# Two diffusion blocks on one core: new due times for the instruction planner, and two unread products at TensorE's start

## The chip, the cores and the metric

The kernel runs on one core of a Trainium2 chip. The metric is the device time of one execution in microseconds. A core has five engines that run side by side, each with its own queue of instructions in a fixed order: TensorE (PE in the profile; PEld is its weight load), VectorE (DVE), ScalarE (ACT), GpSimd (POOL) and SyncE (SP), which here only issues transfers. They wait for one another through semaphores. TensorE writes its products into eight banks of PSUM, called W here; VectorE and ScalarE read them from there.

## The reference

For each of 16 images of 256 tokens with 256 channels, two transformer blocks are computed in float32, one after the other. Shortened:

```python
# block 1: three residual parts, each modulated by m = silu(cond) @ w_ada + b_ada
h = ln(x) * (1 + sc_msa) + sh_msa
x = x + g_msa * self_attention(h)        # windows of 128 tokens, shifted by 64, 16 heads of 16
h = ln(x) * (1 + sc_mca) + sh_mca
x = x + g_mca * topk_cross(h, ctx)       # softmax over the 16 largest of 256 scores
h = ln(x) * (1 + sc_mlp) + sh_mlp
x = x + g_mlp * (silu(a) * b @ w_m2 + b_m2)      # a, b = halves of h @ w_m1 + b_m1, 1024 each
# block 2: cross attention, both sides normalized and modulated by cond
q = (ada_ln(x, ctx_cond, Wss_q) @ Wq + bq); k, v = ada_ln(ctx, ctx_cond, Wss_kv) @ Wkv + bkv
out = x + softmax(q k^T / 4) v @ Wp + bp
```

The outputs are the 16 images of 256 x 256.

## The kernel before

All weights are loaded once and stay on chip. At the start the conditioning vectors are turned into scales, shifts and gate rows: `conditioned` loads `cond`, makes silu of it on ScalarE and VectorE, turns it with TensorE (line 704) and copies it into the tile `condT`; `ada_columns` multiplies pieces of `w_ada`, which are loaded into tiles named `rest`, with it (line 721) and adds the bias (lines 727 and 729, VectorE); `gate_rows` does the same for the gate rows (lines 742 and 762), which go to memory and come back per image (line 394). `biases` loads the bias vectors and turns them into columns (line 678, copied by VectorE at 679).

Then each image passes through five stages, named by tags: `self` (self attention), `prep` (keys, values and queries of the top-k attention), `topk`, `mlp`, and `last` (block 2). Work of neighbouring images is mixed: while VectorE looks for the 16 largest scores of one image, TensorE works on the feed-forward part of the image before and on the self attention of the image after.

The lines that the prediction speaks of: normalization by `normalized` (BN statistics at 442 and 444 on VectorE, three small operations and the scaling into `xn` on GpSimd at 449 to 454), turned to channel-major at 466 (TensorE) and modulated at 480 (ScalarE) into `xT`; products of `xT` with weights at 492 and 528; self attention scores at 798, their maxima at 605 (VectorE), sent by sixteen small transfers into the query tile at 622 (SyncE, from the transposed maxima `nmT`), scores again at 806, exponentials at 629 (ScalarE), products with the values at 598, division at 555 to 558, back to channel-major at 565, projection at 575 with weights that were multiplied with the gate row at 421 (GpSimd, `gw`). A round of the top-k attention (there are four per image) has scores at 845 into four banks; VectorE then takes, per bank, the eight largest (MAX8, 864), removes them (872), takes the next eight (884) and removes them (889); ScalarE makes exponentials (877), GpSimd multiplies (893) into `prT`, and TensorE turns this at 542 for the product with the values at 598. The feed-forward part is 906 to 933, block 2's scores are 950 and 962.

TensorE takes three kinds of work, with 128, 32 or 33 rows or columns at a time (the `mode` of an operation): 798, 806, 845, 950 and 962 are of the second kind, 598 of the third, the rest of the first.

The order of every engine's instructions is decided before the kernel is built. Each operation has a due time, from the table `DUE` by tag and by its number in the tag, to which the image's number is added. The class `Plan` sorts all operations by due time, hands out tiles and banks in that order, and emits them. The tags `topk`, `self`, `prep`, `last` and `mlp` have one table each for all middle images, so the order there repeats from image to image. The planner also follows a rough time of each engine; where it expects TensorE to wait for over a microsecond, it puts in fillers, which are products of the identity matrix with itself into a free bank that nobody reads:

```python
            if o.eng == "PE" and t - free["PE"] > IDLE and free["PE"]:
                ...
                n = int((t - max(free["PE"], ok[0][0]) - 0.15) / FILLER) if ok else 0
```

What stands ahead of the plan (the identity matrix, masks for even and odd heads made from it, and tiles set to fixed values) is put into the queues by the framework's own scheduler.

Of the kernel before, what the change touches and what calls it, by code (L numbers as in the profile page):

```python
# [12 lines left out]
ALU = mybir.AluOpType  # L13
# [3 lines left out]
P = 128  # L17
# [17 lines left out]
        -9079, -9474, -9247, -7795, -10959, -5686, -7231, -10933, -5595, -5764, -7671, -10944, -8055, -6777, -10987,  # L35
        -8081, -7859, -719, -437, -438, -481, -6999, -7280, -511, -720, -536, -6808, -436, -8602, -467, -7346, -144,
        -528, -1472, -8696, -179, -78, -9103, -26, -462, -493, -574, -8606, 35, 199, -2104, 292, -47, 992, 1098, 1338,
        -644, 26, -8994, -144, 52, 10, -8772, -241, -8701, 551, 74, 19, 1012, -516, -8708, 29, 1085, 1257, -514, -452,
        -6996, 1627, 1833, 1607, 911, 1468, 582, -843, -8601, 1445, 486,
    ),  # L40
    "self0": (
        -199, -1161, -7107, -1119, -1199, -1060, -1485, -9186, -125, -11006, -9245, -9080, -1563, -9248, -3868, -1470,
        -9200, -1606, -6831, -7277, -7299, -7349, -1217, -6958, -8697, -6883, -8698, -8665, -312, -310, -2158, -3486,
        -3338, -3035, -3750, -1684, -9048, -7290, -1182, -7290, -2158, -3339, -3752, -3826, -3561, -128, -8903, -9100,
        -1236, -8924, 9, -4022, -51,
    ),
    "prep0": (
        -524, -3251, -614, -3532, -3488, 354, -2949, 516, -8780, -39, -37, 80, 196, -3410, 569, -100, -3471,
    ),
    "topk0": (  # L50
        338, 282, 143, 7, -2799, -24, 100, -98, -2853, -35, 73, -8610, -2853, -8623, 112, -8616, -3052, -8436, -261,
        148, 579, -3006, -8621, -8749, 142, 439, -2809, 383, 324, 558, 726, -3356, -8631, -8719, 484, 172, -2951, 700,
        959, 1002, 919, 1061, 392, -8453, 550, -8714, -3364, 156, -461, 619, -3499, -8620, 551, 18, -2986, -61, 600,
        525, 700, 764, 725, 748, 690, -3352, 906, 842, 826, 553, 724, -72, 621, 835, 742, -3579, 803, 913, 816, 1073,
        821, 1081, 1074, 1309, 1219, 1329, 523, 620, 786, 1012, -3363, 1018, 801, 909, -3366, 958, 747, 1071, -3580,
        914, 791, 1170, -3634, 1022, 1024, 929, 1074, 820, 1013, 1016, 882, 1086, 819, 1181, 1178, 1255, 1240, 907,
        1133, 1169, 1256, 1239, 356, 1199, 1303, 1172, 1160, 1328, 1014, 1043, 1101, 1277, -3653, 1038, 1200, 1248,
        409, 1104, 1256, 1284, 352, 1060, 1143, 1107, 820, 1126, 1125, 1086, 972, 1307, 1262, 1260, 1197, 1206, 350,
        1052, 1246, 1188, 1311, 44, 1162, 1262, 1203, 1208, 1113, 1319, 1173, 1303, 1217, 1329, 677, 1356, 1398, 1437,
    ),  # L60
    "self1": (
        -4802, -987, -890, -482, -9103, -2047, -2146, -2225, -1549, -4844, -830, -1228, -5196, -3811, -1470, -4841,
        -4773, -861, -3828, -878, -800, -795, -794, -10252, -1021, -10208, -10029, -9854, -9854, -780, -807, -1214,
        -647, -4386, -4386, -4444, -3942, -602, -1053, -474, -328, -94, -659, -4237, -4066, -4401, -4387, -598, -1062,
        -270, -247, -15, 68, -4369, -213,
    ),
    "prep1": (
        -771, -5058, 71, -4579, -15, -331, -4364, 378, 34, 220, 223, 231, 182, -29, 145, 237, 302,
    ),
    "topk": (  # L70
        75, 3, 189, 110, 62, 3, -90, 2, 110, -39, 146, -53, -991, -146, 143, -62, -955, 353, 414, 558, 675, -104, 128,
        193, 253, 480, -914, 242, 339, 417, 490, -137, 393, 516, 407, 576, 134, 697, 349, 735, 402, 1049, 530, 279,
        443, -349, 556, 186, 562, 282, 1, 362, 587, 185, 11, 298, 611, 223, 479, 184, 179, 630, 712, -106, 253, 325,
        663, 746, 44, 673, 676, 706, 802, 580, 536, 739, 373, 857, 761, 882, 688, 894, 661, 942, 689, 837, 737, 833,
        885, 737, 799, 832, 902, 347, 344, 704, 30, 337, 331, 643, 725, 836, 941, 190, 1036, 1011, 826, 838, 232,
        1029, 960, 745, 776, 746, 903, 907, 736, 760, 415, 902, 909, 1090, 853, 1036, 1144, 1150, 894, 940, 677, 1028,
        721, 964, 206, 947, 922, 899, 675, 1026, 1075, 934, 678, 824, 918, 1039, 1051, 810, 1113, 1056, 691, 992, 779,
        1040, 959, 1033, 1027, 1116, 1109, 854, 1034, 1034, 999, 1107, 1008, 1160, 1027, 956, 1194, 1085, 501, 1236,
        1061, 1158,
    ),  # L80
    "self": (
        -1974, -677, -761, -758, -1718, -1767, -1387, -1242, -787, -1974, -758, -688, -1415, -1974, -694, -590, -601,
        -589, -1833, -538, -566, -1347, -1349, -1348, -345, -418, -466, -472, -473, -465, -226, -194, -253, -935,
        -969, -968, -425, -138, -335, -332, -197, -113, -150, -1139, -298, -295, -227, -133, -256, -227, -162, -70,
        -86, -126, -322,
    ),
    "prep": (
        -13, -197, -211, 5, 112, 57, 324, -19, -554, -568, -220, -220, -131, 617, 6, 17,
    ),
    "last": (  # L90
        1013, 1044, 1117, 1178, 1185, 1226, 6, 1311, 1060, 579, 1353, 1396, 2041, 1826, 1981, 1931, 2094, 1980, 2195,
        2146, 2088, 2131, 2195, 2090, 2231, 1173, 1171, 2258, 2182, 2188, 2187, 2280, 2286, 2324, 2285, 2351, 2342,
        2323, 2365, 2397, 2127, 2172, 2174, 2173, 2438, 2020, 2436, 1144, 1120, 1010, 1009, 2491, 2276, 2527, 2557,
        2522, 1882, 1284, 1283, 1388, 2589, 2220, 2310, 2627, 2557, 2593, 2591, 2133, 2518, 2425, 2647, 2528, 2649,
        2630, 2660, 2404, 2402, 2518, 2500, 2696, 2346, 2343, 2729, 2753, 2837, 2026, 2507, 2778,
    ),
    "mlp": (
        1668, 1326, 1271, 1268, 1484, 1490, 263, 1703, 1600, 1470, 1499, 1559, 1526, 1674, 1632, 1661, 1535, 959, 187,
        1556, 1289, 1565, 387, 1576, 1568, 1509, 398, 1568, 1257, 1602, 1505, 1616, 1614, 1238, 1421, 1717, 1041,
        1735, 1238, 1735, 1861, 1881, 1096, 1599, 1507, 1509, 1880, 1847, 1806, 859, 1648, 1897, 1712, 1861, 1529,  # L100
        1236, 1674, 882, 881, 1669, 1488, 1497, 847, 1474, 1745, 1088, 1027, 1748, 1027, 1396, 1020, 1336, 1944, 1978,
        1824, 2000, 1827,
    ),
    "self15": (
        -1762, -523, -14014, -616, -1736, -1651, -1652, -1042, -1147, -1738, -740, -1095, -1898, -709, -1266, -1267,
        -714, -1266, -347, -461, -328, -681, -998, -682, -328, -692, -173, -199, -712, -536, -370, -134, -249, -135,
        -196, -91, -162, -473, -302, -550, -648, -122, -354, -338, -167, -311, -83, -133, -766, -1659, -1733, -391,
        -316, -531, -392, -89, -90, -132, 9, -79, -1091, 38, -156, 56, 66, 20, 13, -2, -161, 241, -708, 238, -329,
        -330, -707, -708, 285, 291, 352, 224, 380, 268, -316, 172, -317, 101, 373, 359, 179, 337, 398, 481, 119, 495,
    ),  # L110
    "prep15": (
        -222, -967, 42, -45, -151, 164, 74, 16, -18, -558, -561, -12, -92, 162, 74, -25, 404, 542, 547, 120, 490, 572,
        643, 502,
    ),
    "topk15": (
        92, -80, 136, -123, 133, 163, 171, 196, 78, -109, 193, -109, -1023, 159, 130, 159, 158, 168, 185, 236, 271,
        94, 359, 360, 220, 427, -879, 398, 395, 509, 539, 549, 225, 229, 239, 315, 98, 643, 334, 674, 696, 1147, 445,
        592, 580, 515, 622, 396, 473, 393, 135, 439, 492, 151, -117, 197, 491, 200, -720, 603, 393, 670, 731, 644,
        587, 467, 498, 747, 808, 512, 590, 633, 676, 688, 392, 652, 737, 918, 876, 1071, 1261, 1573, -3159, 1602, 662,
        649, 517, 806, 441, 730, 751, 594, 825, 557, 651, 683, 892, 1122, 220, 963, 926, 822, 821, 246, 1476, 1180,  # L120
        657, 1112, 340, 1069, 1260, 833, 878, 299, 1088, 1346, 1180, 703, 174, 1401, 1346, 1595, 1790, 1787, -3140,
        1762, 890, 977, 706, 952, 896, 1190, 230, 1298, 1524, 1092, 707, 1667, 1501, 877, 345, 1190, 1191, 950, 1150,
        486, 1439, 1557, 1723, 1722, -2841, 1673, 2223, 1608, 1749, -2985, 1586, 2177, 693, 1028, 120, 1674, 1645,
        2210, 2346, 2345, -3151, 2194,
    ),
    "last15": (
# [39 lines left out]
LAG = {"PE": 0.22, "DVE": 0.14, "ACT": 0.18, "POOL": 0.1}  # L166

IDLE, FILLER = 1.0, 0.87
ISSUE, BEGIN, LAND, RATE, OPEN = 0.53, 0.9, 0.4, 320.0, 8


class Buf:
# [941 lines left out]
```

## Time and profile before

| | us |
|---|---|
| median of 3 runs | 1350.14 (1349.22 to 1350.87) |
| the profiled execution | 1350.46 |
| its span, first to last instruction | 1348.6 |
| TensorE busy | 1323.5 |
| VectorE busy | 1217.5 |
| GpSimd busy | 1020.9 |
| ScalarE busy | 1014.2 |
| fillers (line 353), 15 in the program, 30 records | 18.3 |

A group in the profile is read as line, engine, operation, output and inputs, sizes, and count. [...] Busy times of matmuls overlap at their ends; so the time from one group's start to the next group's start is the better measure of what a group costs. In brackets behind an instruction stands how long its engine had been idle before it, and what ended that. The fraction after the engines' busy times in a view of stretches is the granted clock of TensorE.

### The profile page before, as it was taken

The page shows a single profiled execution, that of the slowest core. Times are in us where ns is not written, and L with a number is a line of the kernel's source. Part 1 is how long each engine was busy: PE and PEld are TensorE (multiplying, and loading weights), DVE is VectorE, ACT ScalarE, POOL GpSimd, SP SyncE. Part 2 cuts the span into 40 slices and gives each one's busy share as a digit, 9 for nine tenths or more (in the row PEclk, how much of TensorE's full clock was granted, in tenths as well). Part 3 has the DMA queues.
Part 4 walks back from the last instruction along what each step waited for, and adds up shares of the span by engine and source line. Part 5 has one row for each costly group of instructions (what it writes and reads, how often), then busy time and mean ns, then how long its engine had stood idle before and what let it go on. Part 6 is the DMA issues. An engine that isn't in the chain of part 4 may idle for free.

```text
span 1348.6 us, 38673 instructions
## 1 busy us (share of the span) xinstructions
PE 1323.5 (98%) x13494; PEld 1033.3 (77%) x13494; DVE 1217.5 (90%) x4358; ACT 1014.2 (75%) x2359; POOL 1020.9 (76%) x1552
## 2 busy tenths in 40 slices
PE   8889999999999999999999999999999999999998
PEld 6557787878778787887878788787878778787785
DVE  4699999999999999999999999999999999998844
ACT  4356779787887978778787777878777787978774
POOL 1377887879688787968878796887869788877962
PEclk9889999999999999999999999999999999999999
DMA  5430010101001010100101010010101000000000
GB/s 157 139 109 10 26 41 11 41 17 33 18 18 41 11 40 18 34 17 19 41 11 38 20 34 18 18 41 11 38 20 34 18 27 17 18 18 2 17 2 18
DMA packets 64161, 42.45 MB, mean 31 GB/s; under 512 B 37763, under 2 KB 56751, under 8 KB 63711
## 3 DMA queue, kind: packets, MB, share of 16 engines
q1 hardware_dynamic: 63967, 39.99, 10.7%
q8 instruction: 107, 1.75, 0.6%
q14 instruction: 87, 0.71, 0.2%
HBM read 35.14 MB, written 4.29 MB: 29 GB/s over the span
## 4 chain that ended last, share of the span: by engine, by line
PE 92%; DVE 3%; SPq 1%; issue 1%; DMA 1%; ACT 1%; POOL 0%; POOLq 0%; DVEq 0%; ACTq 0%
PE W L906 17%; PE W L492 12%; PE W L598 11%; PE W L542 8%; PE W L933 8%; PE W L528 6%; PE W L575 6%; PE W L950 5%; PE W L845 5%; PE W L962 5%; PE W L466 3%; PE W L806 2%; PE W L798 2%; SPq L622 1%; DVE rest L872 1%
## 5 line engine op out<-in xcount | busy, mean ns | idle before, releaser
L893 POOL TENSOR_TENSOR prT<-rest,prT 128x512 f32<-128x512 f32 x256 | 325.0, 1273 | 75.0 <-DVE rest L889 73.5
L605 DVE TENSOR_REDUCE nm<-W 128x2 f32<-128x512 f32 (+1 forms) x384 | 239.9, 682 | 30.9 <-PE W L798 17.4
L877 ACT ACTIVATE prT<-W,ntop 128x256 f32<-128x256 f32 x512 | 214.2, 491 | 52.2 <-POOL ntop L866 38.8
L906 PE MATMUL W<-xT,w_L_xcond_w_m 128*128 128x256 f32 (+1 forms) x1088 | 249.1, 373 | 0.0
L629 ACT ACTIVATE pTO<-W 128x512 f32<-128x512 f32 (+1 forms) x392 | 198.8, 596 | 41.9 <-PE W L962 28.9
L906 PEld LDWEIGHTS W<-xT,w_L_xcond_w_m 128*128 128x128 f32 x1088 | 187.6, 190 | 52.3 <-ACT pTO L629 10.6
L872 DVE MATCH_REPLACE8 rest<-top,W 128x256 f32<-128x256 f32 x512 | 209.0, 419 | 0.0
L889 DVE MATCH_REPLACE8 rest<-top,rest 128x256 f32<-128x256 f32 x512 | 206.7, 416 | 0.0
L864 DVE MAX8 top<-W 128x8 f32<-128x256 f32 x512 | 190.1, 420 | 15.7 <-PE W L845 12.8
L884 DVE MAX8 top<-rest 128x8 f32<-128x256 f32 x512 | 190.7, 418 | 0.0
L545 ACT ACTIVATE pTT<-W 128x512 f32<-128x512 f32 x256 | 148.7, 622 | 17.2 <-PE W L542 15.2
L542 PE MATMUL W<-ident,prT 128*128 128x128 f32 x1024 | 145.2, 277 | 4.4 <-ACT k L514 1.7
L542 PEld LDWEIGHTS W<-ident,prT 128*128 128x128 f32 x1024 | 117.9, 142 | 27.9 <-issue 6.2
L923 POOL TENSOR_TENSOR mb<-ma,mb 128x256 f32<-128x256 f32 (+1 forms) x136 | 94.8, 697 | 40.1 <-ACT mb L921 24.4
L558 POOL TENSOR_TENSOR on<-tr,rec 128x128 f32<-128x128 f32 (+1 forms) x162 | 71.0, 443 | 67.8 <-DVE rec L557 67.5
L933 PE MATMUL W<-w_L_xcond_w_m,h 128*128 128x256 f32 x512 | 113.7, 379 | 0.0
L933 PEld LDWEIGHTS W<-w_L_xcond_w_m,h 128*128 128x128 f32 x512 | 97.0, 190 | 13.7 <-POOL x L416 0.3
L555 DVE STREAM_TRANSPOSE tr<-W 128x256 f32<-128x256 f32 (+1 forms) x162 | 78.4, 485 | 29.6 <-PE W L598 15.6
L598 PE MATMUL W<-pTO,v 128*17 128x128 f32 (+1 forms) x2112 | 102.2, 323 | 0.0
L926 POOL TENSOR_TENSOR h<-h,mb 128x256 f32<-128x256 f32 (+1 forms) x136 | 94.7, 696 | 8.2
L416 POOL TENSOR_TENSOR x<-x,gated 128x512 f32<-128x512 f32 (+1 forms) x49 | 60.4, 1233 | 40.9 <-ACT gated L415 40.9
L921 ACT ACTIVATE mb<-W,half 128x256 f32<-128x256 f32 (+1 forms) x136 | 64.4, 489 | 31.7 <-PE W L906 31.6
(129 smaller groups left out, 2678.5 us busy)
## 6 DMA issues: line engine op xcount, KB each, us to landing
gate<-gates SPq DMA_DIRECT2D x48, 256.0 KB
q<-nmT SPq DMA_DIRECT2D x480, 1.0 KB
cx<-in_ctx_dram SPq DMA_DIRECT2D x19, 256.0 KB
cx<-in_ctx_dram SPq DMA_DIRECT2D x104, 32.0 KB
rest<-in_L_xcond_w_ada_dram SPq DMA_DIRECT2D x9, 256.0 KB
x<-in_x_dram SPq DMA_DIRECT2D x16, 128.0 KB
x<-in_x_dram SPq DMA_DIRECT2D x32, 64.0 KB
w_L_xcond_w_m<-in_L_xcond_w_m_dram SPq DMA_DIRECT2D x1, 2048.0 KB
```

Source lines behind the costliest of these rows:

```text
L542: nc.tensor.transpose(w.t[:, ts(n, P)], flat[:, ts(n, P)], ident)
L598: nc.tensor.matmul(po.t[ds(NW * j, DH + 1), ds(q0, nq)], v.t[:, kt, 8 * m + 2 * j + a, :], pT.t.rearrange("p n q -> p (n q)")[:, ds(part, ...
L605: op("DVE", 0.61, lambda j=j, s=s: nc.vector.tensor_reduce(nm.t[:, k, ds(j, groups, step=4)], s.t.rearrange("p (g k) -> p g k", g=groups), ...
L629: op("ACT", 0.24 + q * 0.0005, lambda s=s, pT=pT: nc.scalar.activation(pT.t.rearrange("p n q -> p (n q)")[:, :q], s.t[:, :q], AF.Exp), r=[ ...
L864: nc.vector.max(top.t[:, a, 0:8], s.t[:, ts(a, L)])
L872: nc.vector.match_replace(rest.t[:, a, :], top.t[:, a, 0:8], s.t[:, ts(a, L)], TAKEN)
L877: nc.scalar.activation(pr.t[:, a, :], s.t[:, ts(a, L)], AF.Exp, bias=ntop.t[:, a:a + 1])
L884: nc.vector.max(top.t[:, a, 8:16], rest.t[:, a, :])
L889: nc.vector.match_replace(rest.t[:, a, :], top.t[:, a, 8:16], rest.t[:, a, :], TAKEN)
L893: op("POOL", 1.25, lambda: nc.gpsimd.tensor_tensor(pr.t, rest.t, pr.t, ALU.mult), r=[rest, pr], w=[pr])
L906: nc.tensor.matmul(w.t[:, :q], w_m1.t[:, c, ds(n0, P)], xT.t[:, c, :q], start=c == 0, stop=c == NCC - 1)
L933: nc.tensor.matmul(pp.t[:, ts(k, C)], hs[f].t[:, ts(k, P)], w_m2.t[:, f, :], start=f == 0, stop=f == NHC - 1)
```

## The change

Three things change.

1. All tables of due times (`DUE`) have other numbers. With them the order of nearly all operations on all five queues changes a little, and so do the places where the planner puts fillers: 17 instead of 15. In a middle image the stages overlap in much the same way, with a few groups exchanged. Between the second and the third scores of a middle image's top-k rounds, TensorE's groups in the program were

```
before: 906x10 542x4 598x8 962x8 906x6 598x8 798x16 962x8 906x4 542x4
after:  906x14 962x8 542x8 906x2 598x16 798x16 962x8 906x4
```

(line of before, and matmuls of the program). At the start, the order up to the second top-k scores of image 0 was

```
before: ... 575x4 721x4 742x2 762x2 798x16 528x4 466x4 FILL 492x4 466x4 845x4 FILLx2 806x32 528x4 845x4
after:  ... 575x4 492x4 762x2 721x4 798x16 FILL 466x4 798x16 492x4 845x4 528x4 FILLx7 542x4 845x4
```

The loads at the start have another order too: two pieces of `w_ada` come first, `w_co` and `w_q` early.

2. Ahead of the plan TensorE gets two products of 128 x 512 of a tile of ones with itself, into a bank, unread. VectorE sets the tile, the last of the tiles named `rest`.

3. The instructions that make the masks are written behind that memset.

```diff
 DUE = {
     "start": (
-        -9079, -9474, -9247, -7795, -10959, -5686, -7231, -10933, -5595, -5764, -7671, -10944, -8055, -6777, -10987,
+        -8063, -13109, -13393, -10603, -7993, -10430, -7672, -8906, -10758, -5773, -7871, -8977, -10145, -7674, -8976,
...
 IDLE, FILLER = 1.0, 0.87
+WARM = 2
 ISSUE, BEGIN, LAND, RATE, OPEN = 0.53, 0.9, 0.4, 320.0, 8
...
     ones = const.tile([P, 2], F32, name="ones")
-    by_head = ident.rearrange("p (g two d) -> p g two d", two=2, d=DH)
-    by_pair = ident.rearrange("p (g c) -> p g c", c=2 * DH)
-    for par in range(2):
-        nc.vector.tensor_reduce(masks[:, par:par + 1], by_head[:, :, par, :], AX.XY, ALU.add)
-        nc.vector.tensor_reduce(ones[:, par:par + 1], by_pair[:, :, DH * (1 - par):DH * (1 - par) + 1], AX.XY, ALU.add)
-    nc.vector.tensor_scalar(qmasks, masks, QSCALE, None, ALU.mult)
     nc.scalar.activation(ready_now, neg_half[:, 0:1], AF.Exp)
...
         tiles[kind] = [ps.tile([P, 512], F32, name=f"{kind}{n}") for n in range(count)]
+    nc.vector.memset(tiles["rest"][-1], 1.0)
+    by_head = ident.rearrange("p (g two d) -> p g two d", two=2, d=DH)
+    by_pair = ident.rearrange("p (g c) -> p g c", c=2 * DH)
+    for par in range(2):
+        nc.vector.tensor_reduce(masks[:, par:par + 1], by_head[:, :, par, :], AX.XY, ALU.add)
+        nc.vector.tensor_reduce(ones[:, par:par + 1], by_pair[:, :, DH * (1 - par):DH * (1 - par) + 1], AX.XY, ALU.add)
+    nc.vector.tensor_scalar(qmasks, masks, QSCALE, None, ALU.mult)
     for t in tiles["nm"]:
         nc.vector.memset(t, 0.0)
...
     plan.filler = filler
+
+    def warmed():
+
+        z, w = tiles["rest"][-1].rearrange("p a l -> p (a l)"), tiles["W"][-1]
+        for _ in range(WARM):
+            nc.tensor.matmul(w, z[:, :P], z, start=True, stop=True)
     op = plan.op
...
     with tc.manual_schedule():
+        warmed()
         plan.run()
```

## The prediction

> **What bounds the kernel now.** I read the page first (busy shares, slices), then the stretches of the head, then TensorE's instructions in order of time there, then one middle image.
>
> ```profile
> PE 1323.5 (98%) x13494; PEld 1033.3 (77%) x13494; DVE 1217.5 (90%) x4358; ACT 1014.2 (75%) x2359; POOL 1020.9 (76%) x1552
> PE   8889999999999999999999999999999999999998
> DVE  4699999999999999999999999999999999998844
> PEclk9889999999999999999999999999999999999999
> ```
>
> TensorE is the bound, except in the first four and the last slices. The next view gives stretches: length, then busy time of PE, PEld, DVE, ACT and POOL, granted clock, DMA.
>
> ```profile
> 55.43:177.10 121.67, 110.13 (x966) 82.44 (x966) 115.44 (x461) 78.46 (x182) 91.28 (x136) 0.93 0.17 54
> 208.13:287.10 78.97, 78.97 (x822) 62.37 (x821) 75.04 (x267) 62.21 (x144) 63.34 (x95) 1.00 0.10 26
> 59.00:60.00 1.00, 1.00 (x2) 0.48 (x3) 1.00 (x6) 0.64 (x2) 0.21 (x1) 0.50 0.04 9
> ```
>
> 55.43 is image 0's first MAX8, 177.10 image 2's. In that stretch VectorE is busy 115.44 of 121.67 us and TensorE's 110.13 include fillers and half-clock time, so VectorE sets the pace there and idles only 6.23 us. From image 2 on TensorE has 78.97 us of work in 78.97 us: no wait is left, and only its own work and its mode switches can shrink. The head in order of time:
>
> ```profile
> 3.97 2.08 PE L353 MATMUL W<-ident 128*128 128x512 f32 x2
> 6.43 3.80 PE L721 MATMUL W<-condT,rest 128*128 128x128 f32 x16
> ...
> 46.13 1.02 PE L762 MATMUL W<-rest,condT 128*16 128x256 f32 x4 [1.44 <-DMA rest<-in_L_xcond_w_ada_dram]
> ...
> 50.02 0.60 PE L466 MATMUL W<-ident,xn 128*128 128x128 f32 x4
> ...
> 54.27 1.14 PE L845 MATMUL W<-k,q 32*128 32x512 f32 x8
> 58.96 3.78 PE L353 MATMUL W<-ident 128*128 128x512 f32 x4 [3.54 <-ACT prT L877]
> ...
> 67.37 1.14 PE L845 MATMUL W<-k,q 32*128 32x512 f32 x8
> ```
>
> The first top-k scores (L845) come at 54.27, the second only at 67.37, behind L806 (62.67) and L528 (65.44); in between TensorE was idle for 3.54 us and its clock fell to 0.50. VectorE's waits of 54 to 130 us show what that cost:
>
> ```profile
> DVE top L864 <- PE W L845: 4.3, 3, 2.4
> DVE rest L872 <- ACT prT L877: 1.1, 1, 1.1
> ```
>
> (2.4 of the 4.3 is the unavoidable first one.) A middle image, for the price of a mode switch:
>
> ```profile
> 290.98 1.06 PE L598 MATMUL W<-pTO,v 128*17 128x256 f32 x16
> 291.97 1.15 PE L962 MATMUL W<-q,k 32*128 32x256 f32 x16
> ...
> 302.28 1.06 PE L598 MATMUL W<-pTO,v 128*17 128x256 f32 x16
> 303.16 1.06 PE L598 MATMUL W<-pTT,v 128*17 128x128 f32 x32
> ```
>
> Sixteen L598 take 0.99 us to the next start when 32-row work follows, 0.88 when more L598 does: leaving the mode costs 0.11.
>
> **The change part by part.** The sum is made against the profiled execution: 1350.46 us, span 1348.6; the median 1350.14 is 0.32 below it. Counts are from the built programs' instruction lists; up to image 2's first L845 both hold the same real matmuls, and the same again after it, so savings before and after that point add.
>
> *Masks.* In VectorE's list the six instructions (about 0.9 us from 5.11) stand where they stood, behind the BN statistics; only the memset of ones moves in front. The row of condT (128x256, 0.27) bounds it at 0.27 to 0.54; VectorE idles 1.39 us before 2.80, which hides it. Without that cover it would cost the 0.54. Nothing.
>
> *The two products.* They can start at about 1.3 (VectorE begins at 0.80, plus memset). The two fillers at 58.96 took 3.71 us at clock 0.50, so 1.86 each: the products end at 5.0 (3.0 at full clock, 0.86 each). Queued behind them is L704, which ran at 3.68: 1.3 later. Then 0.3, a filler of 0.86 to 1.86, and L721 begins at 7.1 instead of 6.43. Against that the clock. L721 took 0.23 us each at 6.43, 0.11 to 0.13 later in the head, so the half pace held until about 9.7, although the record reads 1.00: 6.05 us after TensorE's start at 3.68. The same 6.05 from 1.3 is 7.35; sixteen L721 then take 2.0 instead of 3.63 and end at 9.1. L678 now stands behind them (0.27) and with it the bias copy and the shift, so L492 follows 1.95 after instead of 1.30: 11.05 against 11.36, -0.3. Bounds: -0.9 (clock already up, then the second load of rest, which let L721 go on only at 8.48 before, issued 0.8 earlier now) and +1.4 (half pace throughout, L721 to 10.8). The clock's later falls and rises (57.5, 64.3; 101.9, 105.3) lie 6.8 and 3.4 apart. In the Trainium skill, "TensorE: Matmul & The Clock Gate" (Part 1) has a free-running window of 3.4 us that must be busy throughout before the clock rises: two products of 3.7 us guarantee no full one, which speaks against them, and with the work behind them the rise would fall anywhere from 4.7 to 8.1, 6.4 in the middle; by that L492 is at 10.9, and the sum 0.15 better.
>
> *Up to the first L845.* Between, the chain is scores, maxima, sixteen DMA issues (L622, 23.13 to 32.73), L806, and it is unchanged; SP's queue ahead of it holds 36 transfers instead of 35 and 0.43 MB more, which at the 0.2 to 0.4 MB/us that the stretches of 8 to 19 us moved delays it by 0 to 1.4, mostly hidden since SP was done at 22.3: +0.4. Behind it, the gate row's load (L394) loses the load of rest in front of it (0.5 of SP): -0.45 on gw, on L575 and on x. TensorE reached L466 at 50.02 because L762 had waited 1.44 for a load and two groups stood ahead; xn was there at 48.65. Now L762 reads a tile loaded before the L622s, and after L575 (42.3) come 1.73 + 0.97 + 1.1 + 1.1 + a filler 0.87: 48.1, then xn rules. What is late next is rest3 for L721, up to 1.0. So L466 is 0.4 to 1.5 earlier beyond the shift; I take 1.5 less than before in all: with +0.4 and -0.3, L845 at 52.9, **-1.4** (bounds +0.7 and -2.8).
>
> *The VectorE stretch.* L528 and seven fillers (7 x 0.86 = 6.0 us) now follow the first L845, and the second L845 comes right after the first transposes, about 11 us behind the first, while VectorE needs 11.7 for a round (55.43 to 67.1): its idle 1.41 at 67.1 goes. TensorE also doesn't fall to half clock there; VectorE was busy through those slices, so that frees TensorE time but no end by itself. Of the other 4.8 us of idle I take a quarter, since all queues are reordered: **-2.6**. Bounds: -6.2 (all idle gone), and +3.2, three more waits like the 1.07 for prT.
>
> *Middle images.* Each of 13 periods has 30 mode switches instead of 31: two L598 groups between the second and third L845 become one, taking out a 128-to-33 and a 33-to-32 switch and adding a 128-to-32. Four L542 take 0.53 (290.45 to 290.98) when L598 follows, 0.43 when 128-row work does: 0.10 for the first; the second is the 0.11; the added one 0.10 (L906, 0.96 against 0.86 for four). Net -0.11, times 13: **-1.4** (bounds 0 and -2.7, two switches). A new wait is a rival.
>
> *Tail.* 146.9 us from image 15's first L845, with seven fillers instead of five. In waits they cost nothing; on the path 2 x 0.86. Against that, 32 L598 now run together where 16 of them had stalled (2.38 for 0.99, at 1317.77). **0** (bounds -1.5 and +2).
>
> Sum: -1.4 - 2.6 - 1.4 = -5.4, from 1350.46 to 1345.1; against the median 1344.7. I take 1344.9.
>
> **The rivals.** (1) The plan's gain in the head doesn't come: reordered queues put other waits where the 1.41 was, and the DMAs eat the start. For it: VectorE idles only 6.23 us there and POOL and ACT feed it. Against: the second L845 is plainly earlier. Then -1.4 for the periods and -0.4: 1348.6, no change. (2) Slower: a wait in every middle image. All queues are reordered, TensorE has none now, and each 0.1 us costs 1.3. The group moved furthest is the fourth round's L542, from 14.6 us behind the second L845 to about 8; its producer on POOL ended at 367.75, and the new place would be at 372.6, a margin of 4.9; the third has 2.2. So rather not; but a wait of 1.03, like that of L542 for prT at 72.33, times 13 is +13.4: 1358.3. It decides from (5.4 + 2.7)/13 = 0.62 us per image. (3) The products only delay: clock late, L492 at +1.4 instead of -0.3: 1346.6, still faster.
>
> **How the numbers follow.** About 0.2% (2.7 us) is what a measurement here can tell from no change. My forecast, (3) with it, gets 0.68, (1) 0.18, (2) 0.14. The likeliest case alone spans 1341 to 1347.4. The range adds rival (1) and a small wait of (2): 1341.0 to 1351.5, leaving out 0.06 below (most VectorE idle gone and a better tail) and 0.12 above.
>
> **What would show it.** The first L845 near 52.9; the second about 11 us behind; no clock of 0.50 from 57 to 64; VectorE idle of some 3.6 us between the first MAX8 of images 0 and 2; a middle period of 78.86; the stretch from image 15's first L845 to the end near 146.9. Wrong if the middle period is over 79.4, if L492 starts after 12, or if VectorE idles 6 us or more.

## The result and the profile after

The changed kernel takes 1361.04 us (median of 4 runs, 1360.32 to 1363.62) where before took 1350.51 beside it: 1.0078 of before, 95% interval 1.006 to 1.0097. It is slower by 10.5 us; I had forecast 5.4 faster, in a range that ended at 1351.5. The profiled execution took 1363.62 us, span 1361.8, and is 2.6 us above the median.

In the changed kernel the lines behind the masks are 11 higher than in the kernel before: L492 is L503, L528 L539, L542 L553, L598 L609, L721 L732, L845 L856, and so on. The page of the changed kernel, busy time and slices:

```profile
PE 1326.9 (97%) x13502; PEld 1031.3 (76%) x13502; DVE 1217.8 (89%) x4359; ACT 1012.7 (74%) x2359; POOL 1024.3 (75%) x1552
PE   9878999999999999999999999999999999999998
DVE  4698999899999999999999999999999999999844
PEclk9989999999999999999999999999999999999999
```

Nothing in it looks different: a loss of 0.8% is invisible at this resolution. The stretches show it (from image 0's first MAX8 to image 2's; image 3's period and a usual middle period, both from first scores to first scores; the clock between the first and the second scores):

```profile
56.24:180.21 123.97, 108.16 (x991) 81.80 (x994) 115.50 (x462) 78.81 (x182) 87.56 (x131) 0.96 0.16 50
257.61:340.13 82.52, 80.66 (x822) 62.99 (x821) 75.20 (x270) 62.15 (x144) 63.56 (x95) 0.98 0.10 24
659.38:738.92 79.54, 79.17 (x821) 62.23 (x820) 75.20 (x270) 62.14 (x144) 63.42 (x95) 1.00 0.10 25
58.00:64.00 6.00, 6.00 (x15) 2.46 (x13) 6.00 (x26) 3.75 (x9) 0.89 (x4) 1.00 0.01 2
```

The middle period was 78.97 us long with 78.97 of TensorE; now it is 79.54 with 79.17, so TensorE waits. VectorE's head stretch is longer too, 123.97 for 121.67, with 8.47 us idle for 6.23. The head in order of time (a matmul of the program has two records: the four L365 are the two products):

```profile
1.44 3.78 PE L365 MATMUL W<-rest 128*128 128x512 f32 x4 [1.44 <-DVE rest L343]
...
6.88 1.95 PE L732 MATMUL W<-condT,rest 128*128 128x128 f32 x16
...
47.74 1.16 PE L732 MATMUL W<-condT,rest 128*128 128x128 f32 x8 [1.81 <-DMA rest<-in_L_xcond_w_ada_dram]
...
55.08 1.14 PE L856 MATMUL W<-k,q 32*128 32x512 f32 x8 [0.56 <-ACT q L514]
...
57.99 6.17 PE L358 MATMUL W<-ident 128*128 128x512 f32 x14
...
65.66 1.14 PE L856 MATMUL W<-k,q 32*128 32x512 f32 x8
```

The products do what they should (sixteen L732 take 1.95 us, before 3.80), with the fillers the clock stays up (1.00 from 58 to 64, before 0.50 from 59 to 60), and the second scores follow the first by 10.6 us instead of 13.1; but the first scores are at 55.08, before 54.27. TensorE's longest waits over the whole span, changed kernel (in all, how often, the longest):

```profile
PE W L553 <- ACT xT L491: 4.9, 7, 1.7
PE W L732 <- DMA rest<-in_L_xcond_w_ada_dram: 4.0, 2, 2.1
PE W L553 <- POOL prT L904: 3.7, 5, 1.3
```

Where the 13.2 us between the two profiled spans lie, by the first top-k scores of an image (in us; the last two columns are kernels of the experiments):

| | before | changed | cx first (experiment 1) | weights later too (experiment 7) |
|---|---|---|---|---|
| first product of w_qkv | 11.36 | 11.77 | 10.95 | 10.20 |
| image 0's first scores | 54.27 | 55.08 | 54.09 | 52.34 |
| image 0's to image 2's | 121.78 | 123.28 | 121.28 | 121.34 |
| image 2's to image 14's | 948.01 | 958.67 | 945.31 | 945.29 |
| image 14's to image 15's | 77.68 | 77.80 | 77.79 | 77.80 |
| image 15's to the end | 146.86 | 146.97 | 146.93 | 146.93 |
| span | 1348.6 | 1361.8 | 1345.4 | 1343.7 |

10.66 of the 13.2 come from twelve middle periods; nine are 79.25 to 79.68 long, three longer (82.52 for image 3, in which the clock fell for a time; 80.69, 80.36). The head adds 2.3, image 14's period and the tail 0.1 each.

What TensorE waits for is seen by going back from L553, which turns prT. First SP in one period of the kernel before, then in one of the changed kernel (start, duration, issues):

```profile
563.55 0.39 SPq L374 DMA_DIRECT2D cx<-in_ctx_dram  x1
564.04 1.66 SPq L368 DMA_DIRECT2D x<-in_x_dram  x3
568.01 0.33 SPq L394 DMA_DIRECT2D gate<-gates  x1
```

```profile
642.05 1.88 SPq L379 DMA_DIRECT2D x<-in_x_dram  x3
656.31 0.33 SPq L405 DMA_DIRECT2D gate<-gates  x1
656.73 0.39 SPq L385 DMA_DIRECT2D cx<-in_ctx_dram  x1
```

SP's wait in that period, and VectorE's waits for cx over the whole span, both of the changed kernel:

```profile
SPq L405 <- POOL gated L441: 12.3, 1, 12.3
DVE st L453 <- DMA cx<-in_ctx_dram: 14.7, 13, 2.5
```

The load of cx, for the keys of an image's last attention, now stands behind the load of a gate row. That one waits 12.3 us for POOL to release a gate buffer, so cx goes out at 656.73, 2.7 us before the image's first scores at 659.38; before, it went out at 563.55, 7.5 us ahead of those at 571.08. In the same period of the changed kernel, VectorE, POOL, ACT and TensorE in order of time:

```profile
660.63 0.75 DVE L453 BATCH_NORM_STATS2 st<-cx 128x6 f32<-128x256 f32 x2 [1.00 <-DMA cx<-in_ctx_dram]
...
662.34 0.21 POOL L877 TENSOR_SCALAR ntop<-top 128x2 f32<-128x2 f32 x1 [0.84 <-DVE top L875]
...
662.59 0.84 ACT L888 ACTIVATE prT<-W,ntop 128x256 f32<-128x256 f32 x2 [1.28 <-POOL ntop L877]
663.32 1.02 ACT L491 ACTIVATE xT<-W,ada_shift_q,ada_scale_q 128x256 f32<-128x256 f32 x2
...
664.49 0.63 PE L553 MATMUL W<-ident,prT 128*128 128x128 f32 x4 [0.22 <-ACT xT L491]
665.27 0.66 PE L553 MATMUL W<-ident,prT 128*128 128x128 f32 x4
```

VectorE's statistics of cx stand ahead of the new scores' maxima and wait 1.00 for the load; the maxima begin 2.13 us after the scores (before 1.16), POOL's ntop and ACT's softmax (L888) wait for them, ACT's xT stands behind L888, and TensorE's L553 waits for the bank that xT reads. The chain of waits of the changed kernel says it shortest, in image 3, where the load took longest (start, duration):

```profile
254.96 5.37 DMA cx<-in_ctx_dram
260.35 0.75 DVE st L453 x2
```

A transfer on the chain, in a stage where before nothing but TensorE was.

### The profile page after: what moved, and what is told of

Read it like the earlier page. It is cut to its first block, busy times and chain, and to the rows that moved or that the text cites. A ratio compares the mean times of both kernels' runs of the same rounds, so it can differ in the third digit from the quotient of the medians.

```text
span 1361.8 us, 38649 instructions
## 1 busy us (share of the span) xinstructions
PE 1326.9 (97%) x13502; PEld 1031.3 (76%) x13502; DVE 1217.8 (89%) x4359; ACT 1012.7 (74%) x2359; POOL 1024.3 (75%) x1552
## 3 DMA queue, kind: packets, MB, share of 16 engines
q1 hardware_dynamic: 63967, 39.99, 10.6%
## 4 chain that ended last, share of the span: by engine, by line
PE 74%; DVE 9%; POOL 5%; DMA 3%; issue 2%; ACT 1%; SPq 0%; POOLq 0%; DVEq 0%; ACTq 0%
PE W L917 16%; PE W L503 9%; PE W L609 9%; PE W L553 7%; PE W L944 5%; PE W L586 5%; PE W L973 5%; PE W L961 4%; PE W L539 4%; PE W L856 3%; POOL prT L904 3%; PE W L817 2%; DVE top L875 2%; DVE rest L883 2%; PE W L477 2%; PE W L809 2%
## 5 line engine op out<-in xcount | busy, mean ns | idle before, releaser
L888 ACT ACTIVATE prT<-W,ntop 128x256 f32<-128x256 f32 x512 | 214.4, 497 | 100.5 <-POOL ntop L877 76.0
L917 PEld LDWEIGHTS W<-xT,w_L_xcond_w_m 128*128 128x128 f32 x1088 | 188.6, 190 | 41.0 <-ACT pTO L640 10.6
L875 DVE MAX8 top<-W 128x8 f32<-128x256 f32 x512 | 188.1, 416 | 13.5 <-PE W L856 13.1
L895 DVE MAX8 top<-rest 128x8 f32<-128x256 f32 x512 | 185.4, 411 | 0.0
L556 ACT ACTIVATE pTT<-W 128x512 f32<-128x512 f32 x256 | 151.8, 619 | 30.9 <-PE W L553 27.2
L553 PE MATMUL W<-ident,prT 128*128 128x128 f32 x1024 | 149.1, 279 | 15.1 <-ACT xT L491 4.9
L553 PEld LDWEIGHTS W<-ident,prT 128*128 128x128 f32 x1024 | 114.3, 141 | 54.6 <-POOL ntop L877 11.5
L569 POOL TENSOR_TENSOR on<-tr,rec 128x128 f32<-128x128 f32 (+1 forms) x162 | 71.3, 444 | 52.9 <-DVE rec L568 52.6
L934 POOL TENSOR_TENSOR mb<-ma,mb 128x256 f32<-128x256 f32 (+1 forms) x136 | 94.8, 698 | 13.2 <-ACT mb L932 10.9
L609 PE MATMUL W<-pTO,v 128*17 128x128 f32 (+1 forms) x2112 | 98.7, 323 | 0.0
L877 POOL TENSOR_SCALAR ntop<-top 128x2 f32<-128x2 f32 x256 | 55.1, 216 | 47.1 <-DVE top L875 46.5
```

The lines of the kernel that those rows point to most:

```text
L553: nc.tensor.transpose(w.t[:, ts(n, P)], flat[:, ts(n, P)], ident)
L609: nc.tensor.matmul(po.t[ds(NW * j, DH + 1), ds(q0, nq)], v.t[:, kt, 8 * m + 2 * j + a, :], pT.t.rearrange("p n q -> p (n q)")[:, ds(part, ...
L875: nc.vector.max(top.t[:, a, 0:8], s.t[:, ts(a, L)])
L888: nc.scalar.activation(pr.t[:, a, :], s.t[:, ts(a, L)], AF.Exp, bias=ntop.t[:, a:a + 1])
L895: nc.vector.max(top.t[:, a, 8:16], rest.t[:, a, :])
L917: nc.tensor.matmul(w.t[:, :q], w_m1.t[:, c, ds(n0, P)], xT.t[:, c, :q], start=c == 0, stop=c == NCC - 1)
```

## The experiments

All change due times or leave the two products out; all compute everything. Ratios are to the kernel before, run beside them.

**1. The load of cx ahead of the gate row.** One number; the lists of TensorE, VectorE, ACT and POOL stay what they are in the changed kernel.

```diff
     "last": (
-        1090, 985, 1185, 1150, 1185, 1208, 227, 1400, 324, 551, 1423, 102, 2053, 1504, 1457, 1640, 2120, 2032, 2174,
+        1078, 985, 1185, 1150, 1185, 1208, 227, 1400, 324, 551, 1423, 102, 2053, 1504, 1457, 1640, 2120, 2032, 2174,
```

> One due time of the changed kernel is altered: the load of cx for an image's last attention goes from 1.090 to 1.078 periods, so that on SP it stands ahead of the gate row's load (due 1.079) instead of behind it. The instruction lists of all other engines stay as they are. Theory A (the load of cx is the cause): in the changed kernel SP issues the gate row's load only when POOL's L441 has released a gate buffer, and the load of cx stands behind it (656.73 in one period, where before it was at 563.55 of a period that began at 492.1); so VectorE's statistics of cx (L453) wait 0.7 to 2.5 us in 12 middle images, the first MAX8, POOL's ntop, ACT's softmax and ACT's xT (L491) come late by as much, and TensorE stops in L553 for a bank that xT has not read out. By it these waits go (14.7 us of VectorE's waits for cx, 4.9 of TensorE's for xT, both to under 1), the middle period falls from 79.3-79.6 to 78.9-79.0, the long periods (80.4 to 82.5) go, and the time falls from 1361 to 1352.5 (1351 to 1354). Theory B (the order on ACT is the cause: one more L888 stands ahead of xT, wherever cx lands): L888 goes on waiting for ntop, the period stays at 79.3 or more, and the time at 1358 or more.

Measured: 1348.33 us (before 1349.84), ratio 0.9989 (0.9977 to 1.0, so not clearly faster than before). No statistics wait for cx, and TensorE's waits between image 2's first scores and image 15's are gone. SP and TensorE in one period, and the period:

```profile
632.54 0.54 SPq L385 DMA_DIRECT2D cx<-in_ctx_dram  x1
644.85 0.33 SPq L405 DMA_DIRECT2D gate<-gates  x1
```

```profile
650.91 1.89 PE L539 MATMUL W<-w_L_xcond_w_kv,xT 128*128 128x256 f32 x8
652.64 1.04 PE L553 MATMUL W<-ident,prT 128*128 128x128 f32 x8
```

```profile
647.91:726.67 78.76, 78.76 (x822) 62.34 (x821) 75.18 (x270) 62.18 (x144) 63.38 (x95) 1.00 0.10 26
```

The gate row still waits 12 us, with nothing behind it now. Set against the changed kernel, TensorE gains 0.38 at the first L553 after the scores and 0.78 by the next product, and no more in the rest of the period: the whole of 79.54 - 78.76 lies in that one place. About half of it is idle time in the changed kernel's profile (79.54 - 79.17), the other half stands there as longer busy time (79.17 for 78.76). Theory A holds, and more came back than I expected (1351 to 1354): the period fell below that of before, and the 14.7 us of VectorE's waits cost about 12 us (0.9% of the time).

The Trainium skill, "DMA: Bandwidth & Descriptors", section "Anatomy of one DMA — SWDGE (gpsimd) path", says that DMA engines wait on no semaphore: the wait happens on the issuing sequencer before dispatch. That section is about transfers issued through GpSimd, and these are issued by SP; the two listings of SP agree with it: between 643.9 and 656.3 SP issued nothing, though the load of cx behind the waiting one could have gone, as experiment 1 shows, where it left at 632.54.

**2. Without the two products.**

```diff
-WARM = 2
+WARM = 0
```

> The changed kernel without its two products of ones (the memset and all due times stay). Theory A (the products quicken the clock, but the next matmuls wait for the weights w_qkv): L732 runs at half pace again and ends after 10.5, L503 begins at 11.8 to 12.6 instead of 11.77, and the time is 0 to 0.8 us longer than that of the changed kernel: 1361 to 1361.8. Theory B (the products hold up the start, since L715 stands behind them): L715 comes before 4.2 instead of 5.15, L503 no later than 11.8, and the time is the same or up to 1 us shorter.

Measured: 1361.88 us, ratio 1.0088 (1.0075 to 1.0101), with the products 1.0078 (1.006 to 1.0097). The sixteen L732 began at 6.24, L503 at 11.51 after a wait of 0.65 for w_qkv, image 0's first scores came at 54.56 (changed kernel 11.77 and 55.08). Without the products the start was not later, contrary to A, and L715 came at 3.67, as B had it; the times do not tell the two apart. In this kernel w_qkv lands late either way; experiment 8 asks what the products are worth where it lands earlier.

**3. Products and masks with the due times of before.** Every table of due times is the one of before.

```diff
 DUE = {
     "start": (
-        -8063, -13109, -13393, -10603, -7993, -10430, -7672, -8906, -10758, -5773, -7871, -8977, -10145, -7674, -8976,
+        -9079, -9474, -9247, -7795, -10959, -5686, -7231, -10933, -5595, -5764, -7671, -10944, -8055, -6777, -10987,
...
```

> The two products and the moved masks with the due times of before: the part of the change that is not the due times. Theory A (the clock comes up earlier, and the load of w_qkv decides how much of that is kept): the first product of w_qkv, at 11.36 before, begins between 10.5 and 11.4, what follows moves with it until the next load, and the time is 1349.5 to 1350.5 (within 0.1 per cent of before). Theory B (products and masks are themselves to blame for a part of the loss): over 1352.

Measured: 1348.93 us (before 1349.84), ratio 0.9991 (0.9982 to 1.0001). The first product of w_qkv came at 10.74 without a wait for its load, the first scores at 53.65 (before 54.27), the periods at 78.97. In the profiles the first scores are 0.6 us earlier; the times cannot tell that from nothing. B falls: that part of the change is to blame for nothing. The loss is in the due times.

**4. The due times of before for the head alone** (the tables start, self0, prep0, topk0, self1 and prep1 are those of before, the rest those of the changed kernel).

```diff
 DUE = {
     "start": (
-        -8063, -13109, -13393, -10603, -7993, -10430, -7672, -8906, -10758, -5773, -7871, -8977, -10145, -7674, -8976,
+        -9079, -9474, -9247, -7795, -10959, -5686, -7231, -10933, -5595, -5764, -7671, -10944, -8055, -6777, -10987,
...
     "prep1": (
-        -3383, -12384, -382, -14527, -14561, -526, -14844, -920, 211, -175, -20, -88, 205, -14355, 153, 192, 351,
+        -771, -5058, 71, -4579, -15, -331, -4364, 378, 34, 220, 223, 231, 182, -29, 145, 237, 302,
...
```

> The changed kernel with the due times of before for the head (the tables for the start, for image 0 and for the first half of image 1), and its own for the middle images and the tail. The order of SP's loads in the middle images is that of the changed kernel. Theory A (two separate losses: 2.3 us until image 2's first top-k scores and 8 to 10 behind it): image 2's first scores come at 175 to 177 instead of 178.36, VectorE still waits for cx in every middle image, the periods stay at 79.3 or more, and the time is 1357.5 to 1359.5. Theory B (the middle images are late because the head leaves them so): the periods fall to 79.0 and the time to 1351 to 1353.

Measured: 1369.47 us, ratio 1.0148 (1.0133 to 1.0163); both expectations missed it. Image 0's first scores came at 53.93, image 1's at 111.21, but image 2's only at 186.57: two plans that don't fit meet in image 1, and the 75.36 us between its scores and image 2's (62.00 in the changed kernel) say nothing about either head. What can be read is the middle: VectorE waits for cx 0.5 to 1.9 us in each of twelve images and the periods are 79.2 to 80.4 long, though this head is another. That speaks against B.

**5 to 7. Loads of weights later in the head**, on top of experiment 1, in steps. 5 moves w_m2 (start, 1 MB) behind the gate rows' loads; 6 also w_m1 (2 MB) behind the last pieces of `rest`; 7 also w_co and w_q behind w_so. Only SP's list changes. The steps together (-120 is 5, 1133 is 6, the other two are 7):

```diff
-        -10507, -1008, -4676, -2042, -10719, -1776, -2063, -10721, -4677, -4686, -2571, -2591, -10339, -1462, -10384,
-        -2489, -10584, 277, 1198, 1076, 1292, -114, -65, -10181, -150, -1491, -68, -10180, 384, -10475, 1133, -120,
+        -10507, -1008, -4676, -2042, -10719, -1776, -2063, -10721, -2000, -2010, -2571, -2591, -10339, -1462, -10384,
+        -2489, -10584, 277, 1198, 1076, 1292, -114, -65, -10181, -150, -1491, -68, -10180, 384, -10475, 1240, 278,
```

> The kernel of the first experiment (cx ahead of the gate row) with one more move on SP: the load of the 1 MB weight w_m2, issued at 38.39 directly ahead of the two loads of rest, goes behind the gate rows' loads (about 51). All other engines keep their lists. Theory A (transfer order: the DMA engines are full from 38 to 46 us, share 0.96 to 1.05, and the load of rest for L732 waits behind w_m2): L732's wait of 1.68 at 46.75 goes, L477 comes at 48.2 to 49.0 instead of 49.9, the first top-k scores (L856) at 52.4 to 53.2 instead of 54.09, where my prediction had 52.9, and the time falls by 0.9 to 1.7 against the first experiment, in the same share of before to 1346.7 to 1347.5. Theory B (the load of rest is late because its buffer comes free late, at 40): L732 still waits over 1 us, the first scores stay at 54, the time at 1348 to 1349.

Measured: 1347.2 us (before 1349.66), ratio 0.9978 (0.997 to 0.9987). L732 no longer waits, and the first scores come 1.6 us earlier than in experiment 1. TensorE in experiment 5:

```profile
45.16 1.16 PE L732 MATMUL W<-condT,rest 128*128 128x128 f32 x8
...
48.31 0.60 PE L477 MATMUL W<-ident,xn 128*128 128x128 f32 x4
...
52.50 1.14 PE L856 MATMUL W<-k,q 32*128 32x512 f32 x8 [0.56 <-ACT q L514]
```

For the wait and the first scores theory A holds: `rest` was behind 1 MB that nobody needed before image 0's feed-forward. But in the profile the lead of 1.6 us was gone again by image 2's first scores, 176.09 for 175.37 in experiment 1: two groups of eight L503, at 68.40 and 103.15, took 3.07 and 3.67 us where the same groups took 1.93 and 1.99 in experiment 1, the second of them with a granted clock of 0.50 (from 104 to 106). The median is where A had it, but the two intervals overlap, so the gain in time is not shown.

> As the one before, and the load of the 2 MB weight w_m1 (issued at 86.0 ahead of two loads of rest) goes behind them too. Theory A (transfer order decides here too): L732's wait of 2.40 at 97.34 goes, and with it most of VectorE's wait of 2.67 for ACT's prT at 102.92, since the softmax stands behind what TensorE was late with; image 2's first scores come at 171 to 173.5 instead of 175.37, and the time is 1344 to 1346.5 against a before of 1349.8. Theory B (VectorE's wait there comes from the order on ACT or POOL): VectorE's wait stays over 2 us, image 2's scores move only by what the first move gave, and the time equals that of the run before within 0.5 us.

Measured: 1343.74 us, ratio 0.9953 (0.9937 to 0.9968). L732's wait of 2.4 to 2.7 for `rest` became one of 0.75 for ACT, VectorE's wait of 2.67 for ACT's prT 0.2, and image 2's first scores came at 174.12 (experiment 1 175.37, experiment 5 176.09). The interval lies below that of experiment 5. Theory A holds, but for the place: they were expected by 173.5.

> As the one before, and the loads of w_co and w_q (issued at 6.9 to 8.1, needed at 28 and 51 us) go behind that of w_so (about 18). Theory A (they take the transfer time of w_qkv): L503's first wait for w_qkv, 0.26 in the first experiment and 1.32 in the changed kernel, goes, L503 begins by 10.7, and the time falls by 0.2 to 1.0 more: 1343.5 to 1346. Theory B (w_qkv, issued at 4.83 before them, is served before them anyway): L503 stays at 10.9 to 11.8 and the time the same.

Measured: 1343.15 us, ratio 0.9953 (0.9937 to 0.9969), no different from experiment 6. L503 came at 10.20 after a wait of 0.18; in experiments 5 and 6, without this step, at 11.08 and 10.69. In experiments 10, 11 and 12 the same order of these loads gave a wait of 1.16, of 0.15 and none. So the landing of w_qkv varies by about a microsecond from one execution to the next whatever stands behind it, and what the third step is worth stays unclear. This kernel beats both the kernel before and the changed one.

**8. The kernel of experiment 7 without the products.**

```diff
-WARM = 2
+WARM = 0
```

> As the one before, without the two products of ones. Theory A (once the load of w_qkv no longer decides, the early clock counts): the first sixteen L732 take 3.6 us instead of 2.0, L503 begins 0.6 to 1.2 later, all that follows as well, and the time is 0.5 to 1.2 us longer than with the products. Theory B (something else decides the start, a load or the chain on VectorE): L503 within 0.3 of the run with the products, and the time the same.

Measured: 1345.86 us, ratio 0.9968 (0.9954 to 0.9981), with the products 0.9953. Sixteen L732 took 3.66 us, with them 1.95; L503 came at 11.49 (10.20) and the first scores at 53.21 (52.34). That is 0.87 us at the first scores, as A had it, but it compares one execution with one. The repeat of experiment 7 (experiment 12, with the products) had L503 at 10.70 and its first scores only at 53.66, later than here without them: L732 waited 1.24 us for `rest` at 24.89 (0.92 at 23.95 in experiment 7) and L586 0.63 for gw (0.25). For A speaks that executions with the same granted clock, 0.997, spanned 1344.0 to 1345.0 us without the products and 1341.3 to 1342.9 with them (experiments 7 and 12, three in all); against it, that the shortest span of all, 1340.2 at 1.000, is one without them. The two intervals overlap: the products may gain about a microsecond here, but it is not shown.

**9. The converse in the kernel before**: one due time puts the gate row ahead of cx there.

```diff
-        -1974, -677, -761, -758, -1718, -1767, -1387, -1242, -787, -1974, -758, -688, -1415, -1974, -694, -590, -601,
+        -1974, -677, -990, -758, -1718, -1767, -1387, -1242, -787, -1974, -758, -688, -1415, -1974, -694, -590, -601,
```

> The converse, in the kernel before: one due time of its table (the gate row's load for the first half of an image, from -0.761 to -0.990 periods) puts that load ahead of the load of cx on SP, as in the changed kernel. The other engines keep their order; only numbers of PSUM banks differ. In the kernel before SP issued cx at 563.55 and the gate row at 568.01, when POOL had released its buffer. Theory A: cx is now issued behind it, at about 568.4, and lands 3 to 4 us later (3.9 in the changed kernel), at 571.5 to 572.3, while VectorE wants it at 570.26: a wait of 1.2 to 2 us in 12 or 13 middle images, TensorE's bank waits come back behind the image's first scores, the period grows by 0.4 to 1.6 us, and the time by 5 to 21: 1355 to 1371. Theory B (the slip only hurts in the order of the changed kernel, where ACT's L888 stands ahead of xT; before has slack there): VectorE waits for cx, but the period stays under 79.2 and the time under 1353.

Measured: 1372.05 us, ratio 1.0162 (1.0141 to 1.0182): 22 us, from one load that moved past another. VectorE's and TensorE's waits and a period of this kernel (lines as before):

```profile
DVE st L442 <- DMA cx<-in_ctx_dram: 27.0, 12, 2.6
```

```profile
PE W L542 <- POOL prT L893: 11.8, 15, 1.0
```

```profile
579.82:660.64 80.82, 79.55 (x821) 62.15 (x820) 75.03 (x268) 62.34 (x144) 63.37 (x95) 1.00 0.09 25
```

Each of twelve images waits 2.0 to 2.6 us and its period is 1.5 to 2.3 longer, both more than A had (1.2 to 2, 0.4 to 1.6; the time is just over its 1371): the price is about 0.8 us of time per microsecond of VectorE's wait, in an order of ACT and POOL that is not the changed kernel's. Theory B, that only the new order is hurt by a late cx, falls.

**10. Experiment 7 with cx left behind the gate row.** Against experiment 7:

```diff
     "last": (
-        1078, 985, 1185, 1150, 1185, 1208, 227, 1400, 324, 551, 1423, 102, 2053, 1504, 1457, 1640, 2120, 2032, 2174,
+        1090, 985, 1185, 1150, 1185, 1208, 227, 1400, 324, 551, 1423, 102, 2053, 1504, 1457, 1640, 2120, 2032, 2174,
...
```

> The changed kernel with the three moves of the head's weight loads (w_m2, w_m1, w_co and w_q later on SP) but with cx still behind the gate row. Theory A (two independent losses that add): the first scores at 52.3 to 52.6 and image 2's at 173.5 to 175 as with cx moved, the middle periods again 79.3 to 79.6 with some over 80, and the time 10.5 to 13 longer than with cx moved as well: 1354 to 1356.5. Theory B (one hides the other): under 1352 or over 1359.

Measured: 1356.71 us, ratio 1.0046 (1.0029 to 1.0063), against 0.9953 to 0.9959 with cx first: 12 us for the one place in SP's queue, as in experiment 1. First scores at 52.46, periods 79.2 to 79.5 and three over 80. Two losses that add, as A had it, with the time just over its 1356.5; image 2's first scores, at 176.11, were later than expected.

**11 and 12. Two due times for POOL in the head, and experiment 7 again.**

```diff
     "topk0": (
...
-        -8128, 169, 744, -13511, 753, 903, 1287, 1221, 1301, 536, -8081, 173, -8082, -13841, -7912, 661, -7993,
+        -8128, 169, 744, -13511, 753, 903, 1283, 1221, 1301, 536, -8081, 173, -8082, -13841, -7912, 661, -7993,
...
-        632, 847, -13693, -8285, 426, 742, 822, -13903, -8304, -8263, 401, 912, -13658, 1134, 1203, 1298, 1160, 1322,
+        632, 847, -13693, -8285, 426, 742, 822, -13903, -8304, -8263, 401, 912, -13658, 1134, 1203, 1283, 1160, 1322,
...
```

> The kernel with cx ahead of the gate row and the weights later (label e7_late_mq), with two due times of the head's top-k table lowered (1.287 and 1.298 to 1.283), so that on POOL the scaled outputs (L569) of image 0's last scores stand ahead of a normalisation that belongs to image 3, and on VectorE their reciprocals ahead of its statistics. TensorE, ACT and SP keep their order (bank and buffer numbers differ). It asks why the stretch between the first scores of images 0 and 2 stays at 121.3 us although its old waits are gone. Theory A (the stretch is bound by the chain through TensorE, ACT and POOL there, and VectorE's idle time only shows where that chain is read): VectorE's wait of 2.10 for POOL's L569 at 110.68 shrinks to 0.7 to 1.2, but its next wait, for TensorE's L609 (0.75 at 112.05), grows by as much, image 1's first scores stay at 111.9 and image 2's at 173.4 to 173.9, and the time is that of the run without it within 0.5 us. Theory B (each microsecond of VectorE's idle time in this stretch is one of the end, as my prediction counted): image 2's scores and the end come 0.9 to 1.4 earlier.

> The kernel of label e7_late_mq again, beside the other of this pair on the same chip. Both theories: 1342.5 to 1345 where before is 1349.8, image 2's first scores at 173.4 to 174.2.

Measured: 1345.2 us, ratio 0.9956 (0.9944 to 0.9969), and for the repeat 1345.34, ratio 0.9959 (0.9945 to 0.9973): no difference, as A had it. But in its profiled execution image 2's first scores came at 170.95, in the repeat's at 175.05, and the stretch from image 0's was 118.46 us instead of 121.39, more than B had. The two profiles differ in the clock as well. First the repeat, then experiment 11, the same eight matmuls behind the same wait:

```profile
102.27 3.68 PE L503 MATMUL W<-xT,w_L_xcond_w_q 128*128 128x256 f32 x8 [1.11 <-ACT xT L491]
```

```profile
99.87 1.99 PE L503 MATMUL W<-xT,w_L_xcond_w_q 128*128 128x256 f32 x8 [1.11 <-ACT xT L491]
```

1.7 us of the 2.9 are half-clock time that one execution had and the other had not. The rest would fit the two due times (VectorE's wait of 2.10 for POOL is gone), but one profile is no proof, and the times show no gain: executions with a granted clock of 0.997 spanned 1342.0 to 1343.6 us in experiment 11 and 1341.3 to 1342.9 in 7 and 12. What the two due times are worth stays open.

## Why the prediction was wrong

- **Middle images, "a new wait is a rival": this step failed.** It cost +10.7 us over twelve periods where I had -1.4 over thirteen. I had named the mechanism, a wait in every middle image, and given it 0.14, but I judged it by the one group that was moved furthest on TensorE (the fourth round's L542, margin 4.9), and that group never waited. I priced SP's queue in the head only and never compared its order in a middle image, where a load that was ready had been put behind one that was not. The rows for it were there: before, cx left 6.7 us ahead of its reader (563.55 to 570.26) and the gate row, at 568.01, went out when POOL released its buffer. Behind it, cx could not leave before 568.4 and had 1.9 us left, where the load takes 3.6 us or more to reach its reader in the changed kernel. Experiments 1, 9 and 10 show the cause from both sides. The rival's turning point, 0.62 us per image, was passed: 0.68 in a usual period against the 78.86 I had forecast, and more in three.
- **Middle images, the mode switch: right in kind, half in size.** With cx in time the period is 78.76, 0.21 below before, where I had 0.11. From start to start, one L598 group fewer gives 0.13 of it (9.45 us for 9.58); L466 (0.11) and L528 (0.09) give the rest, less 0.10 more in L492.
- **The two products: L732 right, L492 wrong.** I had the sixteen L732 ending at 9.1; they ended at 8.8, and from 8.3 to 9.7 in the experiments with the products. But L492, predicted at 11.05, then waited 1.32 for w_qkv, a load that I did not list among what is late next. My bounds (-0.9 to +1.4) held it. Against "Masks: nothing" experiment 3 shows nothing, though it does not test the masks alone.
- **First scores at 52.9: failed by a transfer.** They came at 55.08: 0.7 from the start, the rest from L732, for which I allowed "up to 1.0" of waiting for rest3. It waited 1.81, because w_m2 was ahead of it on full DMA engines (busy share 0.98 to 1.10 from 38 to 46 us). With that load later they came at 52.50 (experiment 5).
- **The VectorE stretch, -2.6: failed as a step.** The idle time I named (1.41 at the second scores) went, and the scores followed by 10.6 (predicted 11), with no half clock from 57 to 64. But the stretch was 123.28 from scores to scores in the changed kernel, 121.3 with all loads mended, 121.78 before. VectorE's idle time there was 6.23 before, 8.47 changed, 6.27 in experiment 1, 6.06 in experiment 7: it moved, from waits for TensorE's scores to waits for ACT's prT, POOL's L569 and TensorE's L609. I had counted a wait that ends as time that is gained. (The 177.10 that I gave for image 2's first MAX8 before is 0.11 early: it began at 177.21, which changes nothing here.) What holds the stretch at 121.3 (the clock's falls, or the order on POOL) stays open after experiment 11.
- **Tail: right**, 146.97 for 146.9.
- By my own marks the prediction was wrong on two of three: the middle period over 79.4, VectorE idle over 6; L492 at 11.77 stayed under 12.

The sum of -5.4 is close to what the same tables give once three loads (experiment 6) or five (7 and 12) are in order: 5.5 to 6.3 us off before (0.9959 to 0.9953). That is in part luck, since the parts came otherwise: in experiment 7's profile the first scores gave -1.9 (I had -1.4), the stretch -0.4 (-2.6) and the middle images -2.7 (-1.4).

## What to carry to other kernels

Where due times are worked out anew, compare every queue in one steady period, the one that issues the loads first: a ready load behind a waiting one is a wait for all that reads it, and it costs once per image, while the head costs once. Take for each load the time from its issue to its reader in the old profile, and ask when it could leave in the new order. In the head, put large weights that are needed late behind the small pieces that TensorE waits for.

## What the runs showed that I had not expected

The time of the same program differs by several microseconds from execution to execution, and the granted clock with it: twelve executions of experiment 1 spanned 1343.6 us at a mean granted clock of 0.999, 1343.8 to 1345.4 at 0.997, 1346.3 to 1348.2 at 0.996, and 1347.9 to 1350.5 at 0.995 and 0.994. And the clock's rise at the start does not come at the same place in the work: the two fillers behind the products took 1.15, 1.27, 1.57, 1.83 and 2.08 us in five executions with the same start (experiments 7 and 6, the changed kernel, experiments 1 and 5), which, between 1.02 at full pace and 2.08 at half, puts the rise, by my estimate, anywhere from 5.7 us to 7.6. The Trainium skill, "TensorE: Matmul & The Clock Gate", Part 1, calls the window free-running and the number of slow matmuls variable from run to run; these five agree. In experiment 10 the clock rose earlier still: the products themselves took 3.43 us instead of 3.78.

The landing of a load varied as well: cx took 3.6 to 4.0 us from issue to reader in nine periods of the changed kernel, 5.4 in image 3, 5.1 in image 5 and 4.5 in image 13, and these three have the long periods. Image 13's was long in every kernel with a late cx (80.4 in experiments 2, 4 and 10 too); which others were long differed.
